# Selective scan on one core: softplus' sum on TensorE, dt's two projections side by side, preparation one group earlier, one more product with B on GpSimd

## The chip, the cores and the metric

The kernel runs on one core of a Trainium2 chip. The time is that of one execution on the device, in microseconds. A core has four engines that compute: TensorE (PE in the profile; its weight loads are PEld), VectorE (DVE), ScalarE (ACT) and GpSimd (POOL). SyncE (SP) issues the DMA transfers here. Each engine takes its instructions in the order in which the program has them, and waits on semaphores for the others.

## What is computed

The input is 2 images of 128 channels and 64 x 64 pixels. Four layers follow each other: attention, a block of deformable convolutions, a residual block of convolutions, and a selective scan (Mamba) over the pixels in four directions. The change lies in the fourth layer. For one direction, with L = 4096 pixels, 256 inner channels and 16 states:

```python
xz = x @ W_in.T;  xh, z = split(xz)
xh = silu(causal_conv4(xh) + conv_b)
x_dbl = xh @ W_xp.T                      # dt (8), B (16), C (16)
dt = softplus(dt @ W_dt.T + b_dt)
h  = exp(dt * A) * h + dt * B * xh       # the scan, for 256 channels x 16 states
y  = (sum over states of h * C + xh * Dp) * silu(z)
out = y @ W_out.T                        # then the fuse over the four directions, and the residual
```

A layernorm over the channels stands ahead of it.

## The kernel before

`layer3` works in 64 blocks (2 images, 4 directions, 8 blocks of 512 pixels each). The 128 partitions of a scan hold 32 channels times 4 states, so a block is cut into 8 groups: two halves of the channels (`hf`) by four quarters of the states (`ng`). A group has four parts `q` of 32 channels each.

For a group k the work is:

- `weights(k)` (L1347): TensorE spreads B's four rows over the partitions, into a PSUM tile `pbc`; the pool `psb` has two such buffers.
- `db_dve(k)` (L1361): VectorE multiplies `pbc` with dt*xh for the first `ND` = 3 of the four parts, into `db` (128 x 1536). `db_pool(k)` (L1368): GpSimd does the fourth (128 x 512), from a copy of B in SBUF that DMAs have spread (`copies`, L1355).
- `expo(k, q)` (L1375): ScalarE forms exp(dt*A) into a PSUM tile `da`, of which there are three buffers; it runs two scans ahead.
- `scan(k, q)` (L1384): VectorE's scan instruction, four in a group. `keep` (L1390) saves the last state on ScalarE.
- `cmul(k, 0)` and `cmul(k, 1)` (L1395): GpSimd multiplies with C, two parts at a time. `sums(k)` (L1401, L1403): TensorE adds the states into `py`. After four groups `gate` (L1412) multiplies with silu(z) on VectorE.

Beside block i's scans the next block is prepared. One iteration of the loop at L1544 is one group ("slot" 0 to 7 in a block), and in each the helpers `transfers`, `front_pe`, `front_act`, `front_pool` and `next_norm` put in their piece. Everything is in program order (`tc.manual_schedule`): the order of these calls is the order of the queues. The pieces, with their slots before:

| piece | engine | slot before |
|---|---|---|
| `begin`: `conv(i+1, 0)`, and `conv(i+1, 1)` (L1261) | TensorE | 6, 7 of the block before |
| `conv_silu` (L1266), with two table loads | ScalarE | 0 |
| `xproj` (L1285), `xproj_copy` (L1291, L1293) | TensorE, ScalarE | 1 |
| `bc_store` (L1297), B and C to DRAM | SP | 2 |
| `delta(0)`, `delta(1)` (L1311): dt's projections, 8 rows each | TensorE | 2, 3 |
| `softplus(0)`, `softplus(1)` (L1317 to L1320): relu(x) and ln(1 + exp(-abs(x))), into two halves of `dd` | ScalarE | 2, 3 |
| `spread(0)`, `spread(1)` (L1325 the sum of the two, L1326 the product with xh) | GpSimd | 3, 4 |
| `xproj_rest`, `rest_copy` (L1303, L1304, L1307) | TensorE, ScalarE | 4 |
| `spread_store` (L1331), `spread_load` (L1340) | SP | 4 and 5; 5 and 0 |
| `zproj` (L1273), `zproj_silu` (L1279), with two table loads | TensorE, ScalarE | 5 |
| `project` (L1420, L1422), `finish` of the block before | TensorE, ScalarE | 3, 4 |
| the layernorm of image 1: `ln_mean` (L1188), `ln_square` (L1199, L1200), `ln_var` (L1204), `ln_scale`, `ln_store` | TensorE, VectorE and ScalarE, TensorE, ScalarE and GpSimd, ScalarE | 6, 7, and 0, 1, 2 of the next block |

The layernorm of image 1 is done beside blocks 22 to 29, one eighth of the image in each. That of image 0 stands ahead of the first block, after some products that prepare weights.

[...]three for `da` (pool `psd`), two for `pbc` (`psb`, which the weight preparation at the layer's start uses too), one for `py`, and two of the pool `psm` (`pm3`), which all other products take in turn, the layernorm's among them. A buffer of a pool is taken in turn, and the writer waits until the reader of its earlier content is done.

Of the kernel before, what the change touches and what calls it, by code (L numbers as in the profile page):

```python
# [10 lines left out]
F32 = mybir.dt.float32  # L11
# [9 lines left out]
P = 128  # L21
NB = 2
HW = 64
L = HW * HW
BLK = 512
NBLK = L // BLK
# [8 lines left out]
DTR = 8  # L35
# [1067 lines left out]
def layer3(g, I, out):  # L1103
# [5 lines left out]
    nc, tc = g.nc, g.tc  # L1109
    NJ = 4  # L1110
    ND = 3
    NNG = N_STATE // NJ
    HB = 3
    with ExitStack() as ctx:
# [8 lines left out]
        nc.sync.dma_start(winz, I["winzT"])  # L1123
        wxp = a.tile([P, 2, 40], F32, name="wxp")
        nc.sync.dma_start(wxp, I["wxpT"])
        wdt = a.tile([40, 2, P], F32, name="wdt")
        nc.sync.dma_start(wdt[32:40], I["wdtT"])
        am = a.tile([P, 2, 4, NNG], F32, name="am")
# [54 lines left out]
        N = {}  # L1183


        def ln_mean(b, k):
            N[k, "mean"] = psm.tile([P, BLK], F32, name="pm3")
            nc.tensor.matmul(N[k, "mean"], onesm, interior(g, b, k * RB, RB), start=True, stop=True)  # L1188
# [13 lines left out]
        def ln_var(b, k):  # L1202
            N[k, "var"] = psm.tile([P, BLK], F32, name="pm3")
            nc.tensor.matmul(N[k, "var"], onesm, N[k, "sq"], start=True, stop=True)  # L1204
# [34 lines left out]
        NBK = len(blocks)  # L1239
        S = {}  # L1240
# [41 lines left out]
        def xproj(i):  # L1282
            S[i]["px"] = px = psm.tile([P, BLK], F32, name="pm3")
            for hf in range(2):
                nc.tensor.matmul(px[:40, :], wxp[:, hf, :], S[i]["u"][:, hf, :], start=(hf == 0), stop=(hf == 1))  # L1285

        def xproj_copy(i):

            px = S[i].pop("px")
            S[i]["xd"] = ck.tile([40, BLK], F32, name="xd", bufs=1)  # L1290
            nc.scalar.copy(S[i]["xd"], px[:40, :])  # L1291
            bc = S[i]["bc"] = ck.tile([4 * N_STATE, BLK], F32R, name="bc")
            nc.scalar.copy(bc[0:32], px[0:32, :])  # L1293
# [12 lines left out]
        def rest_copy(i):  # L1306
            nc.scalar.copy(S[i]["bc"][32:64], S[i].pop("pl")[0:32, :])  # L1307

        def delta(i, hf):
            pdt = S[i]["pdt", hf] = psm.tile([P, BLK], F32, name="pm3")  # L1310
            nc.tensor.matmul(pdt, wdt[32:40, hf, :], S[i]["xd"][32:40], start=True, stop=True)  # L1311

        def softplus(i, hf):
# [43 lines left out]
        def db_dve(k):  # L1357
            i, hf, ng = groups[k]
            x, n = G[k], ND
            x["db"] = wk.tile([P, 4, BLK], F32, name="db")  # L1360
            nc.vector.tensor_tensor(  # L1361
                x["db"][:, :n, :], x.pop("pb").unsqueeze(1).to_broadcast([P, n, BLK]), S[i]["d4", hf][:, 1, :n, :], ALU.mult
            )

        def db_pool(k):
            i, hf, ng = groups[k]
            x, n = G[k], ND
            nc.gpsimd.tensor_tensor(  # L1368
                x["db"][:, n:, :], S[i]["b", ng].unsqueeze(1).to_broadcast([P, 4 - n, BLK]), S[i]["d4", hf][:, 1, n:, :], ALU.mult
            )  # L1370
# [79 lines left out]
        def front_act(i, slot):  # L1450
            if i < NBK:
                if slot == 0:
                    conv_silu(i)
                elif slot == 1:
                    xproj_copy(i)
                elif slot == 2:
                    softplus(i, 0)
                elif slot == 3:
                    softplus(i, 1)
                elif slot == 4:  # L1460
                    rest_copy(i)
                elif slot == 5:
                    zproj_silu(i)


        def transfers(i, slot):
            if i < NBK:
                if slot == 2:
                    bc_store(i)
                elif slot == 4:  # L1470
                    spread_store(i, 0)
                elif slot == 5:
                    spread_load(i, 0)
                    spread_store(i, 1)
            if slot == 0 and i - 1 < NBK:
                spread_load(i - 1, 1)
            for x, ahead in (("b", 3), ("c", 1)):
                j, ng = divmod(8 * (i - 1) + slot + ahead, 8)
                if ng < NNG and 0 < j < NBK:
                    copies(j, x, ng)  # L1480

        def front_pe(i, slot):
            if i < NBK:
                if slot == 1:
                    xproj(i)
                elif slot == 2:
                    delta(i, 0)
                elif slot == 3:
                    delta(i, 1)
                elif slot == 4:  # L1490
                    xproj_rest(i)
                elif slot == 5:
                    zproj(i)
            if i + 1 < NBK:
                if slot == 6:
                    begin(i + 1)
                elif slot == 7:
                    conv(i + 1, 1)
# [5 lines left out]

        LN = {6: ln_mean, 7: ln_square, 8: ln_var, 9: ln_scale, 10: ln_store}

        def next_norm(i, slot):

            for j, s in ((i, slot), (i - 1, slot + 8)):
                b, k = divmod(j, 4 * NBLK)  # L1510
                k -= 4 * NBLK - 2 - NBLK
                if j >= 0 and b + 1 < NB and 0 <= k < NBLK and s in LN:
                    LN[s](b + 1, k)

        with tc.manual_schedule():
# [3 lines left out]
            for t in range(NBLK + 1):  # L1519
                for s in LN:  # L1520
                    if 0 <= t - s // 8 < NBLK:
                        LN[s](0, t - s // 8)
            begin(0)
            conv(0, 1)
            for slot in range(8):
                front_pe(0, slot)
                front_act(0, slot)
                front_pool(0, slot)
# [15 lines left out]
            for k in range(len(groups) + 6):  # L1544
# [129 lines left out]
def _arrays(i):  # L1674
# [26 lines left out]
    for d, (n, s) in enumerate((("offx", slice(0, 9)), ("offy", slice(9, 18)))):  # L1701
# [5 lines left out]
    wxp = l3["W_xp"]  # L1707
    wxp = np.concatenate([wxp[DTR:], wxp[:DTR]])
    a = {
# [9 lines left out]
        "winzT": l3["W_in"][2 * P :].reshape(2, P, P).transpose(2, 0, 1),  # L1719
        "wxpT": wxp.reshape(40, 2, P).transpose(2, 1, 0),  # L1720
        "wdtT": l3["W_dt"].reshape(2, P, DTR).transpose(2, 0, 1),
# [23 lines left out]
```

## Time and profile before

| | us |
|---|---|
| median of 3 runs | 6007.57 |
| lowest and highest | 5999.1, 6009.02 |
| the profiled execution, its time | 6003.65 |
| the profiled execution, its span | 6001.9 |

In the profiled execution the first scan starts at about 2555 us; the 64 blocks take the rest, some 3450 us. Over the span the engines are busy: TensorE 5221.0 us, VectorE 4554.2, ScalarE 3807.3, GpSimd 3701.6.

How to read the views: in the table of groups a row gives line, engine, operation, output<-input with partitions x elements, count, then busy time in us and the mean ns of one, then the idle time of the engine just ahead of these instructions and what ended it. An fp32 product is recorded as two matmul instructions. In the timeline the first two numbers are start and duration in us, "x2" the number of instructions merged, and the bracket is the idle time ahead of them with its releaser. The chain of waits lists start, duration and what ran.

### The profile page before, as it was taken

How to read it: one execution, taken by the hardware profiler on the slowest of the kernel's cores; microseconds unless marked ns; L12 is line 12 of the kernel's file. 1: busy time of each engine (PE TensorE's matmuls, PEld its weight loads, DVE VectorE, ACT ScalarE, POOL GpSimd, SP SyncE). 2: the span in 40 equal slices, each digit the busy share in tenths (PEclk: the TensorE clock that was granted, in tenths of full speed). 3: DMA queues.
4: the chain of work that ended last, by engine and by line, in shares of the span. 5: the costliest groups of instructions: out<-in, count | busy, mean ns of one | idle time of the engine just before them, and what ended most of it. 6: DMA issues, size and time to landing. Idle time of an engine off the chain costs nothing.

```text
span 6001.9 us, 60094 instructions
## 1 busy us (share of the span) xinstructions
PE 5221.0 (87%) x18726; PEld 1662.7 (28%) x18726; DVE 4554.2 (76%) x4262; ACT 3807.3 (63%) x5867; POOL 3701.6 (62%) x2108
## 2 busy tenths in 40 slices
PE   6999999989978689888998888888898888887877
PEld 3333333334444334212222222222222222222221
DVE  5333333355134698499999999999999999999999
ACT  3888888840035411377777766777777777777765
POOL 5111111100010121199999999999999999999999
PEclk9999999999988899888888888888888888888887
DMA  5000001020066200165665556655665556655564
GB/s 152 18 18 18 18 18 32 1 58 1 15 111 110 51 7 0 28 144 135 145 144 133 138 134 145 143 131 135 150 145 132 141 132 145 145 134 137 135 151 106
DMA packets 373049, 575.61 MB, mean 96 GB/s; under 512 B 91080, under 2 KB 145744, under 8 KB 371632
## 3 DMA queue, kind: packets, MB, share of 16 engines
q1 hardware_dynamic: 367408, 563.94, 40.6%
q10 hardware_dynamic: 5312, 7.76, 0.5%
q8 instruction: 149, 2.44, 0.2%
q14 instruction: 180, 1.47, 0.1%
HBM read 482.34 MB, written 89.13 MB: 95 GB/s over the span
## 4 chain that ended last, share of the span: by engine, by line
DVE 45%; PE 38%; DMA 4%; issue 4%; POOL 4%; ACT 2%; SPq 2%; DVEq 0%; ACTq 0%; POOLq 0%
DVE db L1384 31%; DVE db L1361 11%; PE ps L269 10%; PE acc L285 8%; PE m L1034 5%; PE m L548 4%; DMA dd<-dx 2%; POOL db L1395 2%; PE acd L794 2%; PE pm L1261 1%; PE m L508 1%; DVE gt L1412 1%; PE pf L757 1%; PE py L1403 1%; PE pc L645 1%
## 5 line engine op out<-in xcount | busy, mean ns | idle before, releaser
L1395 POOL TENSOR_TENSOR db<-db,c 128x1024 f32<-128x1024 f32 x1024 | 2401.0, 2360 | 80.7 <-ACT hl L1390 67.5
L1384 DVE TENSOR_TENSOR_SCAN db<-da,hl,db 128x512 f32<-128x512 f32 x1792 | 2158.2, 1265 | 53.8 <-ACT da L1375 7.3
L1375 ACT ACTIVATE da<-dd,am 128x512 f32<-128x512 f32 x2048 | 1406.7, 689 | 918.0 <-DVE db L1384 904.0
L275 ACT ACTIVATE e<-ps 128x1024 f16<-128x1024 f32 x1024 | 992.3, 1021 | 134.8 <-PE ps L269 117.7
L1403 PE MATMUL py<-db,fold 128*32 128x512 f32 x4096 | 831.0, 686 | 203.4 <-POOL db L1395 202.9
L1361 DVE TENSOR_TENSOR db<-pbc,dd 128x1536 f32<-128x1536 f32 x512 | 888.2, 1735 | 51.1 <-DMA c<-bx 51.1
L1261 PE MATMUL pm<-xn,wcs 128*128 128x512 f32 x1024 | 722.8, 857 | 30.6 <-DVE xc L1199 17.6
L296 DVE RECIPROCAL rec<-acc 32x512 f32<-32x512 f32 x64 | 214.9, 3358 | 639.6 <-PE acc L285 612.1
L303 POOL TENSOR_TENSOR parts<-parts 32x512 f32<-32x512 f32 x64 | 80.6, 1259 | 975.3 <-DVE parts L302 975.3
L1368 POOL TENSOR_TENSOR db<-b,dd 128x512 f32<-128x512 f32 x512 | 651.2, 1272 | 21.1 <-DMA c<-bx 14.9
L269 PE MATMUL ps<-q,k 32*128 32x512 f32 x4096 | 656.4, 643 | 3.6 <-DVE flag L232 2.8
L285 PE MATMUL acc<-e,v 128*128 128x512 f16 x2048 | 531.3, 382 | 0.0
L1034 PE MATMUL m<-v,u 128*128 128x512 f32 x864 | 376.4, 598 | 51.6 <-DVE v L1003 51.6
L1401 PE MATMUL py<-u,ddp 128*128 128x512 f32 x256 | 183.6, 806 | 232.1 <-DVE gt L1412 231.8
L1347 PE MATMUL pbc<-bc,sel 64*128 64x512 f32 x512 | 284.2, 555 | 83.7 <-DVE db L1361 77.5
L1403 PEld LDWEIGHTS py<-db,fold 128*32 128x32 f32 x4096 | 115.1, 113 | 805.2 <-POOL db L1395 517.5
L1261 PEld LDWEIGHTS pm<-xn,wcs 128*128 128x128 f32 x1024 | 203.6, 209 | 428.8 <-issue 375.8
L1384 DVE TENSOR_TENSOR_SCAN db<-da,db 128x512 f32<-128x512 f32 x256 | 293.3, 1205 | 9.0 <-ACT da L1375 0.7
L285 PEld LDWEIGHTS <-v 128*128 128x128 bf16 x2048 | 158.5, 97 | 510.0 <-issue 388.7
L269 PEld LDWEIGHTS ps<-q,k 32*128 32x128 f32 x4096 | 229.7, 183 | 228.0 <-issue 147.2
L1347 PEld LDWEIGHTS pbc<-bc,sel 64*128 64x128 f32 x512 | 104.8, 205 | 607.6 <-DVE db L1361 306.3
L548 PE MATMUL m<-comb,w 64*128 64x512 f32 (+4 forms) x1296 | 269.9, 575 | 0.0
(311 smaller groups left out, 5734.9 us busy)
## 6 DMA issues: line engine op xcount, KB each, us to landing
dd<-dx SPq DMA_DIRECT2D x1024, 256.0 KB, 6.6
dx<-dd SPq DMA_DIRECT2D x128, 512.0 KB, 7.2
b<-bx SPq DMA_DIRECT2D x1024, 64.0 KB, 5.3
c<-bx SPq DMA_DIRECT2D x1024, 64.0 KB, 2.1
hats<-pos SPq DMA_DIRECT2D x136, 256.0 KB, 9.8
q<-qd SPq DMA_DIRECT2D x32, 512.0 KB, 8.6
w<-in_conv0T SPq DMA_DIRECT2D x18, 288.0 KB, 8.8
xa<-in_x SPq DMA_DIRECT2D x8, 512.0 KB, 9.1
```

Source lines behind the costliest of these rows:

```text
L269: nc.tensor.matmul(ps[:, i, :], k4[h % 2][rows, kb // 4, :], q4[h % 2][rows, qb * BLK : (qb + 1) * BLK], start=True, stop=True,)
L275: nc.scalar.activation(e[:, :n, :], ps[:, :n, :], AF.Exp)
L285: nc.tensor.matmul(acc, v3[b][:, kb, h, :], e[:, i, :], start=(kb == 0), stop=(kb == NS - 1))
L548: yield lambda q=q, dy=dy, src=src, i0=i0, i1=i1: nc.tensor.matmul(m[:, i0 * NF : i1 * NF], w[half, dy, q, x, :], src, start=(dy == KC and ...
L1034: nc.tensor.matmul(m[x], weights[j][:, dy, x, :], v[j][b][:, x, r0 : r0 + RP, :].rearrange("p r i -> p (r i)"), start=(dy == 0), stop=(dy ...
L1261: nc.tensor.matmul(shaped(blk, pu), wcs[:, hf, s, :], window(blk, sgn * s), start=(s == 0), stop=(s == 3))
L1361: nc.vector.tensor_tensor(x["db"][:, :n, :], x.pop("pb").unsqueeze(1).to_broadcast([P, n, BLK]), S[i]["d4", hf][:, 1, :n, :], ALU.mult)
L1368: nc.gpsimd.tensor_tensor(x["db"][:, n:, :], S[i]["b", ng].unsqueeze(1).to_broadcast([P, 4 - n, BLK]), S[i]["d4", hf][:, 1, n:, :], ALU.mult)
L1375: nc.scalar.activation(da, S[i]["d4", hf][:, 0, q, :], AF.Exp, scale=am[:, hf, q, ng : ng + 1])
L1384: nc.vector.tensor_tensor_scan(d1, d0, d1, 0.0 if first else hl[:, hf, ng, q, :], ALU.mult, ALU.add)
L1395: nc.gpsimd.tensor_mul(v, v, S[i]["c", ng].unsqueeze(1).to_broadcast([P, 2, BLK]))
L1403: nc.tensor.matmul(S[i]["y", hf][32 * q : 32 * q + 32, :], fold, G[k]["db"][:, q, :], start=False, stop=(ng == NNG - 1),)
```

## The change

1. `softplus`' two parts are no longer added by GpSimd. `sum_parts` adds them with two products with the identity on TensorE into a `pm3` tile, and `sum_copy` copies it back to `dd` on ScalarE. `spread` keeps the product with xh alone.
2. `W_xp`'s dt rows stand twice in the prepared weights, so that `xproj` gives dt in rows 32 to 39 and again in 64 to 71. `delta(0)` uses the first, `delta(1)` the second, and both are issued in one slot.
3. Preparation is shifted by one group: `conv` to slots 5 and 6, `conv_silu` to 7, `xproj` and `xproj_copy` to 0, `bc_store`, both `delta`s and `softplus(0)` to 1, `sum_parts(0)`, `softplus(1)` and `sum_copy(0)` to 2, `sum_parts(1)`, `sum_copy(1)`, `xproj_rest` and `rest_copy` to 3, `zproj` to 4. `project` and `finish` both go to slot 5, ahead of the preparation.
4. The layernorm's `mean` and `var` tiles come from `psb` (`pbc`) instead of `psm`, and its steps lie in slots 0, 1, 3, 4 and 5 of one block.
5. In the last group of a block (`hf` = 1, `ng` = 3) GpSimd does two of the four products with B instead of one, and VectorE two instead of three.

```diff
-    ND = 3
+    ND = ((3, 3, 3, 3), (3, 3, 3, 2))
...
-        wxp = a.tile([P, 2, 40], F32, name="wxp")
+        wxp = a.tile([P, 2, 72], F32, name="wxp")
         nc.sync.dma_start(wxp, I["wxpT"])
-        wdt = a.tile([40, 2, P], F32, name="wdt")
-        nc.sync.dma_start(wdt[32:40], I["wdtT"])
+        wdt = a.tile([72, P], F32, name="wdt")
+        for hf in range(2):
+            nc.sync.dma_start(wdt[32 + 32 * hf : 40 + 32 * hf], I["wdtT"][:, hf])
...
         def ln_mean(b, k):
-            N[k, "mean"] = psm.tile([P, BLK], F32, name="pm3")
+            N[k, "mean"] = psb.tile([P, BLK], F32, name="pbc")
...
         def ln_var(b, k):
-            N[k, "var"] = psm.tile([P, BLK], F32, name="pm3")
+            N[k, "var"] = psb.tile([P, BLK], F32, name="pbc")
...
-                nc.tensor.matmul(px[:40, :], wxp[:, hf, :], S[i]["u"][:, hf, :], start=(hf == 0), stop=(hf == 1))
+                nc.tensor.matmul(px[:72, :], wxp[:, hf, :], S[i]["u"][:, hf, :], start=(hf == 0), stop=(hf == 1))
...
-            S[i]["xd"] = ck.tile([40, BLK], F32, name="xd", bufs=1)
-            nc.scalar.copy(S[i]["xd"], px[:40, :])
+            S[i]["xd"] = ck.tile([72, BLK], F32, name="xd", bufs=1)
+            nc.scalar.copy(S[i]["xd"], px[:72, :])
...
-            nc.tensor.matmul(pdt, wdt[32:40, hf, :], S[i]["xd"][32:40], start=True, stop=True)
+            r = slice(32 + 32 * hf, 40 + 32 * hf)
+            nc.tensor.matmul(pdt, wdt[r], S[i]["xd"][r], start=True, stop=True)
...
+        def sum_parts(i, hf):
+            ps = S[i]["dt", hf] = psm.tile([P, BLK], F32, name="pm3")
+            for x in range(2):
+                nc.tensor.matmul(ps, g.ident, S[i]["dd", hf][:, x, :], start=(x == 0), stop=(x == 1))
+
+        def sum_copy(i, hf):
+            nc.scalar.copy(S[i]["dd", hf][:, 0, :], S[i].pop(("dt", hf)))
+
         def spread(i, hf):
...
-            nc.gpsimd.tensor_add(dd[:, 0, :], dd[:, 0, :], dd[:, 1, :])
             nc.gpsimd.tensor_mul(dd[:, 1, :], dd[:, 0, :], s_["u"][:, hf, :])
...
-            x, n = G[k], ND
+            x, n = G[k], ND[hf][ng]
...
         def front_act(i, slot):
             if i < NBK:
                 if slot == 0:
-                    conv_silu(i)
+                    xproj_copy(i)
                 elif slot == 1:
-                    xproj_copy(i)
+                    softplus(i, 0)
                 elif slot == 2:
-                    softplus(i, 0)
+                    softplus(i, 1)
+                    sum_copy(i, 0)
                 elif slot == 3:
-                    softplus(i, 1)
+                    sum_copy(i, 1)
+                    rest_copy(i)
                 elif slot == 4:
-                    rest_copy(i)
-                elif slot == 5:
                     zproj_silu(i)
+            if i + 1 < NBK and slot == 7:
+                conv_silu(i + 1)
...
-                if slot == 2:
+                if slot == 1:
                     bc_store(i)
...
         def front_pe(i, slot):
             if i < NBK:
-                if slot == 1:
+                if slot == 0:
                     xproj(i)
+                elif slot == 1:
+                    delta(i, 0)
+                    delta(i, 1)
                 elif slot == 2:
-                    delta(i, 0)
+                    sum_parts(i, 0)
                 elif slot == 3:
-                    delta(i, 1)
+                    sum_parts(i, 1)
+                    xproj_rest(i)
                 elif slot == 4:
-                    xproj_rest(i)
-                elif slot == 5:
                     zproj(i)
             if i + 1 < NBK:
-                if slot == 6:
+                if slot == 5:
                     begin(i + 1)
-                elif slot == 7:
+                elif slot == 6:
                     conv(i + 1, 1)
...
-        LN = {6: ln_mean, 7: ln_square, 8: ln_var, 9: ln_scale, 10: ln_store}
+        LN = {0: ln_mean, 1: ln_square, 3: ln_var, 4: ln_scale, 5: ln_store}
...
+                if i >= 1 and i <= NBK:
+                    if slot == 5:
+                        project(i - 1)
+                        finish(i - 1)
                 front_pe(i + 1, slot)
                 front_act(i + 1, slot)
                 front_pool(i + 1, slot)
-                if i >= 1 and i <= NBK:
-                    if slot == 3:
-                        project(i - 1)
-                    elif slot == 4:
-                        finish(i - 1)
                 if live:
                     next_norm(i, slot)
```

More of the change, by code (lines that the diff above doesn't have):

```diff
@@ L1366, in db_pool @@
             i, hf, ng = groups[k]
-            x, n = G[k], ND
+            x, n = G[k], ND[hf][ng]
             nc.gpsimd.tensor_tensor(
@@ L1503, in front_pool @@
                     spread(i, slot - 3)
-        LN = {6: ln_mean, 7: ln_square, 8: ln_var, 9: ln_scale, 10: ln_store}
+        LN = {0: ln_mean, 1: ln_square, 3: ln_var, 4: ln_scale, 5: ln_store}
         def next_norm(i, slot):
[L1509 to L1513, printed above, removed]
+            b, k = divmod(i, 4 * NBLK)
+            k -= 4 * NBLK - 2 - NBLK
+            if b + 1 < NB and 0 <= k < NBLK and slot in LN:
+                LN[slot](b + 1, k)
         with tc.manual_schedule():
@@ L1520, in layer3 @@
                 for s in LN:
-                    if 0 <= t - s // 8 < NBLK:
-                        LN[s](0, t - s // 8)
+                    if 0 <= t - s // 3 < NBLK:
+                        LN[s](0, t - s // 3)
             begin(0)
             conv(0, 1)
+            conv_silu(0)
             for slot in range(8):
@@ L1707, in _arrays @@
     wxp = l3["W_xp"]
-    wxp = np.concatenate([wxp[DTR:], wxp[:DTR]])
+    wxp = np.concatenate([wxp[DTR:], wxp[:DTR], np.zeros((24, wxp.shape[1]), np.float32), wxp[:DTR]])
     a = {
@@ L1719, in _arrays @@
         "winzT": l3["W_in"][2 * P :].reshape(2, P, P).transpose(2, 0, 1),
-        "wxpT": wxp.reshape(40, 2, P).transpose(2, 1, 0),
+        "wxpT": wxp.reshape(72, 2, P).transpose(2, 1, 0),
         "wdtT": l3["W_dt"].reshape(2, P, DTR).transpose(2, 0, 1),
```

## The prediction

> **What bounds the kernel now.** I began with the busy time by window. The selective scan fills the time from about 2550 us to the end; two of its windows:
>
> ```profile
> core 0: us, PE busy (x) PEld busy (x) DVE busy (x) ACT busy (x) POOL busy (x), PEclk, DMA share, GB/s
> 3000.00:3500.00 500.00, 435.74 (x1080) 105.80 (x1079) 492.04 (x394) 357.71 (x640) 487.73 (x266) 0.86 0.58 138
> 4000.00:4500.00 500.00, 434.81 (x1084) 109.91 (x1076) 486.26 (x390) 354.62 (x639) 485.32 (x267) 0.85 0.60 143
> ```
>
> VectorE and GpSimd are both busy 97 to 98% of it, so this view alone cannot say which one sets the pace. The chain that ended last, over one block of eight groups, can:
>
> ```profile
> by line: DVE db L1384 64.3%; DVE db L1361 29.8%; issue 5.1%; DVE gt L1412 4.2%; DVEq L1361 0.4%; DVEq L1384 0.3%
> ...
> 5735.93 0.58 DVE gt L1412
> 5736.52 1.68 DVE db L1361
> ...
> 5738.28 2.07 DVE db L1384 x2
> 5740.35 0.31 issue
> 5740.66 2.43 DVE db L1384 x2
> 5743.09 1.66 DVE db L1361
> ...
> 5744.84 2.07 DVE db L1384 x2
> ```
>
> It never leaves VectorE. A group is four scans and one product with B: from 5738.28 to 5744.84, 6.56 us. A block is 8 x 6.56 + 2 x 0.58 (gates) = 53.64 us, and by the starts of the gate rows, read over the whole scan, the blocks follow each other every 53.74 us, nearly all of them. What VectorE loses is lost to the end, what it saves is saved. Next come the groups' rows:
>
> ```profile
> L1395 POOL TENSOR_TENSOR db<-db,c 128x1024 f32<-128x1024 f32 x1024 | 2401.0, 2360 | 80.7 <-ACT hl L1390 67.5
> L1375 ACT ACTIVATE da<-dd,am 128x512 f32<-128x512 f32 x2048 | 1406.7, 689 | 918.0 <-DVE db L1384 904.0
> L1361 DVE TENSOR_TENSOR db<-pbc,dd 128x1536 f32<-128x1536 f32 x512 | 888.2, 1735 | 51.1 <-DMA c<-bx 51.1
> L1368 POOL TENSOR_TENSOR db<-b,dd 128x512 f32<-128x512 f32 x512 | 651.2, 1272 | 21.1 <-DMA c<-bx 14.9
> ```
>
> ScalarE idles 904 us behind VectorE (904/64 = 14 us a block). But how late ScalarE may be at one point is another question; one block of the timeline of VectorE and ScalarE shows it:
>
> ```profile
> 4230.62 0.69 ACT L1266 ACTIVATE u<-pm,vecs 128x512 f32<-128x512 f32 x1 [3.13 <-PE pm L1261]
> ...
> 4233.35 2.46 DVE L1384 TENSOR_TENSOR_SCAN db<-da,hl,db 128x512 f32<-128x512 f32 x2 [3.20 <-ACT da L1375]
> ```
>
> There ScalarE waited 3.13 us for a convolution, and VectorE lost 3.20 us. So **the exps run only two scans ahead**: where ScalarE's extra work for the next block already fills the gap, a wait of ScalarE goes to VectorE in full.
>
> **The skill.** The Trainium skill, page "TensorE: Matmul & The Clock Gate", Part 1, says that the array's clock drops to half after idle time and comes back after some 3.4 us of work. The trace agrees on the halving (how long the return takes it doesn't show): the same dt projection, before and after a stretch with idle gaps of about 1.6 us:
>
> ```profile
> 4072.21 1.12 PE L1311 MATMUL pm<-xd,wdt 8*128 8x512 f32 x2
> ...
> 4080.32 0.79 PE L1347 MATMUL pbc<-bc,sel 64*128 64x512 f32 x1
> 4081.03 2.07 PE L1311 MATMUL pm<-xd,wdt 8*128 8x512 f32 x2
> ```
>
> The same page (head table and Part 3) says that matmuls stay in order, and that ScalarE, VectorE and GpSimd are strict FIFOs; the rows above agree (exps wait behind the late silu). "TensorEngine Tiling (Array Packing)", Overview, has products of few rows on different row groups run together; no run so far shows the two deltas so. "GPSIMD Engine Reference", section 1, has GpSimd contend with VectorE instructions that read two SBUF inputs; db_dve and the scans read one of theirs from PSUM, so I add nothing; no row so far shows it either way.
>
> **The change, part by part.**
>
> *One more product with B on GpSimd.* In one group of eight, db_dve shrinks from 128x1536 to 128x1024. Its slope, from 1735 ns and the gate's 665 ns for 512 elements (timeline rows of L1412), is 1070/1024 = 1.045 ns an element, so 0.535 us a block, on the path: 64 x 0.535 = **-34.2 us**. GpSimd's part grows from 1.272 to 2.36 us (the 128x1024 row), +1.09. It is now due at the third scan instead of the fourth, but db_pool runs a group ahead (5745.31 to 5746.58 for a fourth scan at about 5755), so it has 5 us and more.
>
> *Softplus' sum.* Off GpSimd: two adds of 1.273, -2.55 a block; with the above, -1.46 a block. It was not the bound: nothing gained. Onto TensorE: four fp32 products of 0.92 (the convolution's eight instructions, four products, take 3.70 when warm) = 3.7 us a block. Its bracketed idle times in the block of 5709 to 5763 sum to 10.6, and these cover it. Onto ScalarE: two copies of 0.59 (row L1433), 1.2 of its 14 us. In group 2 it does softplus (2.43) and one copy (0.59), 3.0 in all, less than the 3.87 of conv_silu with two table loads, which delays a scan by 0.06 us today.
>
> *dt's projections side by side.* Two products of 1.05 in one group instead of two; at best 1.0 us of TensorE saved, at worst none; both lie in idle time. xproj with 72 instead of 40 columns streams the same 512 columns, and its copy the same 512 elements: nothing.
>
> *Preparation a group earlier.* conv, conv_silu, xproj_copy, softplus, rest_copy and zproj_silu each come one group sooner, with their producer still one group ahead (or in the same group, as xproj and zproj were). SP's queue: bc_store one group sooner behind its copy; spread_store and all loads (L1340, L1355) keep their groups, behind stores that are ready no later: nothing. project and finish go from groups 3 and 4 to 5, both: TensorE then has project 2.8, begin's convolution 3.7, ddp and sums 3 and weights 0.5 = 10 us in a group of 6.56, a lag of 3.5 us that groups 6 and 7 (5.4 and 1.7) take up before conv_silu and before the weights are due. finish ends some 6 us into the group; the next exp is due at 8.3.
>
> *The layernorm's mean and variance into pbc's two buffers.* This is what I expect to decide. In blocks 22 to 29 (eight blocks) mean comes in group 0 and variance in group 3, each between two weights. With two buffers, mean takes that of the next group's weights, free only when db_dve reads it at the end of the group; and **the weights issued in the group after take the buffer of the weights before mean, free only at the end of that group**. Behind those weights on TensorE stand delta (group 1) and zproj (group 4), and for these ScalarE waits, with the next exps behind it. Before, both lay in psm, and those blocks took 54.6 us (53.74 and the 0.68 of L1199).
>
> Group 1, from its first scan: scans 4.72, gate 0.58, product 1.75: buffer free at 7.05. Weights and first delta, TensorE idle for 4 to 5 us here and in group 4, and thus probably cold: 0.05 + 0.75 + 2.0; warm 0.05 + 0.45 + 1.1. Then softplus 2.43, Square 0.54, exp 0.69: exp at 13.5 cold, 12.3 warm. VectorE wants it at 7.8 + 2.4 = 10.2 (with the layernorm's subtraction). Stall 3.3 or 2.1.
>
> Group 4: buffer free at 6.47; weights 0.8 or 0.5; two products of zproj 3.6 or 1.95; second silu 0.55, table load 1.30, Ln 0.70, Exp 0.53, exp 0.69: 14.6 or 12.7. VectorE wants it at 6.56 + 2.4 = 8.96. Stall 5.7 or 3.7.
>
> Together 9.0 cold, 5.8 warm. I take 8.0, since the last products may be warm again: 8 x 8.0 = **+64 us** (46 to 72).
>
> *The start.* mean now waits behind the weight preparation in the same two buffers (its first product at 2473.65 so far; the preparation's TensorE part is reached at 2480), against a chain whose first variance began at 2480.32: about +2.7. Softplus' last sum goes over TensorE and ScalarE (0.92 to 2 twice, 0.59) instead of an add of 1.27: +1.2 to 3.3. One more DMA of wdt on SP ahead of wfu, which the chain passes: 0.43, within these. **+4.5 us** (2 to 7). At the end project waits for the last gate as before: nothing.
>
> Sum: -34.2 + 64 + 4.5 = +34. Against the profiled execution's 6003.65 us (span 6001.9) that is 6038; the median of the runs, 6007.57, stands 3.9 higher, so 6041.
>
> **The rivals.** (1) *The stall is covered.* If ScalarE's slack or TensorE's lead absorbs the new wait, only the product and the start remain: 6007.6 - 34 + 4.5 = 5978, faster. It decides below (34.2 - 4.5)/8 = 3.7 us of stall per normalising block. For it: the 14 us of ScalarE idle a block. Against it: block 4205 to 4262 above, 3.13 us of wait and 3.20 of loss. (2) *It cancels*: a stall about 4 us, TensorE warm and the Square ahead: 6007.6 - 34 + 32 + 4.5 = 6010. (3) *TensorE becomes the bound* in ordinary blocks: it runs cold part of the time (mean clock 0.85), and the lag of group 5, doubled, could reach conv_silu; 1 us in each of 56 ordinary blocks would be 6041 + 56 = 6097. Against it: 10.6 us idle a block. (4) *The change doesn't do what it says*: the sum on TensorE leaves GpSimd 1.5 us more idle and VectorE as it was; that is in the sum already.
>
> **How the numbers follow.** My case 0.71, mostly 6018 to 6052; rival 1 0.13; rival 2 0.10; rival 3 0.06. Of the likeliest case 0.03 fall within 0.2%, about what a measurement of this kernel can tell from no change (6007.6 +- 12). So slower 0.74, same 0.13, faster 0.13. Leaving out rival 3 and most of rival 1, the range is 5996 to 6062; the likeliest case's own is 6018 to 6052.
>
> **What would show it.** Ordinary blocks 53.2 us from gate to gate, L1361's groups of 128x1024 near 1.2 us. Eight blocks near 62 us, with weights (pbc) waiting for db_dve, softplus and silu waiting for TensorE just after, and two stalls of VectorE behind exps, of about 3 and 5 us. I am wrong if those blocks stay below 57 us, or if ordinary ones exceed 53.7.

## The result, and the profile after

The changed kernel takes 6090.04 us (median of 4 runs, 6085.78 to 6091.52) against 6005.65 (4 runs, 5999.1 to 6009.02): a ratio of 1.0141, 95% interval 1.0123 to 1.0158. The forecast was +34 us; it became +84, beyond the end of the range. Its profiled execution took 6090.28 us (span 6088.5), so the two traces differ by 86.6 us of span.

Busy time by window, the first view of the prediction again, for the changed kernel (the columns are the engines' busy time and instructions):

```profile
core 0: us, PE busy (x) PEld busy (x) DVE busy (x) ACT busy (x) POOL busy (x), PEclk, DMA share, GB/s
3000.00:3500.00 500.00, 424.59 (x1155) 109.30 (x1148) 482.95 (x391) 363.73 (x655) 471.64 (x245) 0.90 0.57 138
4000.00:4500.00 500.00, 405.50 (x1073) 109.46 (x1072) 452.00 (x366) 341.54 (x621) 443.14 (x234) 0.87 0.53 130
```

VectorE was busy 492 and 486 us of these stretches; now it is busy 483 and 452. The engine that set the pace has idle time of 17 us in the first window and 48 us in the second, which holds about half of the layernorm's blocks. The change made VectorE's work smaller and made VectorE wait.

What it waits for is seen in the row of its scans, first before the change, then after it:

```profile
L1384 DVE TENSOR_TENSOR_SCAN db<-da,hl,db 128x512 f32<-128x512 f32 x1792 | 2158.2, 1265 | 53.8 <-ACT da L1375 7.3
```

```profile
L1394 DVE TENSOR_TENSOR_SCAN db<-da,hl,db 128x512 f32<-128x512 f32 x1792 | 2160.5, 1265 | 144.4 <-ACT da L1385 97.6
```

The scans take as long as before, but wait 98 us for ScalarE's exps instead of 7; the 256 scans without an earlier state wait another 15 us (before 0.7). ScalarE's waits have grown as well. More groups of the changed kernel, each shape apart (count | busy, mean ns | idle before, by releaser):

```profile
L1405 POOL TENSOR_TENSOR db<-db,c 128x1024 f32<-128x1024 f32 x1024 | 2401.3, 2358 | 160.4 <-ACT hl L1400 155.5 <-DMA dd<-dx 2.4 <-PE pm L1328 2.0
L1385 ACT ACTIVATE da<-dd,am 128x512 f32<-128x512 f32 x2048 | 1401.9, 689 | 849.7 <-DVE db L1394 845.6 <-DMA c<-bx 0.4
L1371 DVE TENSOR_TENSOR db<-pbc,dd 128x1536 f32<-128x1536 f32 x448 | 778.0, 1737 | 56.0 <-DMA c<-bx 56.0
L1371 DVE TENSOR_TENSOR db<-pbc,dd 128x1024 f32<-128x1024 f32 x64 | 76.7, 1199 | 0.0
L1268 ACT ACTIVATE u<-pm,vecs 128x512 f32<-128x512 f32 x128 | 84.4, 686 | 55.0 <-PE pm L1263 54.3
L1320 ACT ACTIVATE dd<-pm,vecs 128x512 f32<-128x512 f32 x128 | 85.8, 670 | 45.6 <-PE pm L1314 45.6
L1281 ACT ACTIVATE z<-pm 128x512 f32<-128x512 f32 x128 | 70.4, 595 | 39.1 <-PE pm L1275 38.5
```

The smaller product is there, at the forecast size: 64 of 1199 ns beside 448 of 1737. The last three rows are what has grown: conv_silu waits 54 us in all for the convolution (before 16), softplus 46 us for the deltas (before 11), and the silu of z 39 us for zproj (before 1).

Read from gate to gate, the 63 intervals between blocks fall into three kinds. Starts of the first half's gates, in us (the forecast puts the product's 0.535 into every interval):

| stretch | before | after | difference | forecast |
|---|---|---|---|---|
| span's start to first gate | 2591.2 | 2603.0 | +11.8 | +4.5 |
| 28 intervals, preparing a column block | 1503.0 | 1519.9 | +16.9 | -15.0 |
| 8 intervals with the second image's layernorm | 434.6 | 507.4 | +72.8 | +59.7 |
| the 27 others | 1448.9 | 1432.7 | -16.2 | -14.4 |
| last gate to the end | 24.3 | 25.5 | +1.2 | 0 |

Of the 27 others 25 prepare a row block, and two the first column blocks of the second image; they are called row intervals below. Row intervals follow each other every 53.21 us (median; before 53.74), the forecast's 53.2. Column intervals take 54.28 (median; before 53.74). Layernorm intervals take 63.43 on average (before 54.32).

**A layernorm block**, first VectorE's, then TensorE's and ScalarE's rows of its timeline (start, duration, and in brackets the idle time before and its releaser):

```profile
3769.15 2.46 DVE L1394 TENSOR_TENSOR_SCAN db<-da,hl,db 128x512 f32<-128x512 f32 x2 [3.65 <-ACT da L1385]
...
3794.83 2.46 DVE L1394 TENSOR_TENSOR_SCAN db<-da,hl,db 128x512 f32<-128x512 f32 x2 [5.89 <-ACT da L1385]
```

```profile
3762.68 0.76 PE L1357 MATMUL pbc<-bc,sel 64*128 64x512 f32 x1 [3.31 <-DVE db L1371]
3763.37 2.08 PE L1314 MATMUL pm<-xd,wdt 8*128 8x512 f32 x4
...
3786.43 0.79 PE L1357 MATMUL pbc<-bc,sel 64*128 64x512 f32 x1 [4.44 <-DVE db L1371]
3787.15 3.78 PE L1275 MATMUL pm<-xn,winz 128*128 128x512 f32 x4
```

```profile
3765.48 0.69 ACT L1320 ACTIVATE dd<-pm,vecs 128x512 f32<-128x512 f32 x1 [5.64 <-PE pm L1314]
3789.26 0.60 ACT L1281 ACTIVATE z<-pm 128x512 f32<-128x512 f32 x1 [3.68 <-PE pm L1275]
```

This is the chain of the forecast, twice: weights wait for db_dve, deltas (L1314) and zproj (L1275) stand behind them, softplus (L1320) and silu (L1281) wait for those, and the exps behind them come 3.65 and 5.89 us late to a scan. The products after the idle time run slowly: zproj takes 3.78 us here and 1.98 in the row blocks.

**A column block**, which the forecast had not looked at, TensorE's rows, then ScalarE's and VectorE's:

```profile
2869.47 0.49 PE L1357 MATMUL pbc<-bc,sel 64*128 64x512 f32 x1 [1.00 <-DVE db L1371]
2869.90 2.16 PE L1430 MATMUL pm<-xa,ident 128*128 128x512 f32 x2
2871.88 1.90 PE L1432 MATMUL pm<-gt,mt 128*128 128x512 f32 x4
2873.62 7.03 PE L1263 MATMUL pm<-xn,wcs 128*128 128x512 f32 x8
...
2882.44 0.49 PE L1357 MATMUL pbc<-bc,sel 64*128 64x512 f32 x1
2882.86 7.12 PE L1263 MATMUL pm<-xn,wcs 128*128 128x512 f32 x8
...
2890.91 0.49 PE L1357 MATMUL pbc<-bc,sel 64*128 64x512 f32 x1
```

```profile
2890.02 0.69 ACT L1268 ACTIVATE u<-pm,vecs 128x512 f32<-128x512 f32 x1 [0.95 <-PE pm L1263]
```

```profile
2892.74 2.46 DVE L1394 TENSOR_TENSOR_SCAN db<-da,hl,db 128x512 f32<-128x512 f32 x2 [1.01 <-ACT da L1385]
```

In the first two directions of each image the window is a transposed view of xn, and each half of the convolution (four products) takes 7.1 us, not the 3.70 of a row block. Project stands ahead of it with 4 us. The second half ends at 2889.98; the second silu had been ready for it 0.95 us earlier, and VectorE loses 1.01 us.

### The profile page after: what moved, and what is told of

It reads as the page before. It is cut to its first block, busy times and chain, and to the rows that moved or that the text cites. A ratio compares the mean times of both kernels' runs of the same rounds, so it can differ in the third digit from the quotient of the medians.

```text
span 6088.5 us, 61321 instructions
## 1 busy us (share of the span) xinstructions
PE 5237.0 (86%) x19238; PEld 1713.3 (28%) x19238; DVE 4523.5 (74%) x4262; ACT 3862.8 (63%) x5995; POOL 3611.1 (59%) x1980
## 4 chain that ended last, share of the span: by engine, by line
PE 46%; DVE 37%; ACT 6%; issue 4%; DMA 2%; POOL 2%; SPq 1%; DVEq 0%; ACTq 0%; POOLq 0%
DVE db L1394 25%; PE ps L269 10%; DVE db L1371 10%; PE acc L285 8%; PE pm L1263 7%; PE m L1034 5%; PE m L548 4%; PE acd L794 2%; ACT da L1385 2%; PE pm L1430 1%; PE pm L1432 1%; PE m L508 1%; PE pf L757 1%; DVE gt L1422 1%; PE pbc L1357 1%
## 5 line engine op out<-in xcount | busy, mean ns | idle before, releaser
L1371 DVE TENSOR_TENSOR db<-pbc,dd 128x1536 f32<-128x1536 f32 (+1 forms) x512 | 854.7, 1669 | 56.0 <-DMA c<-bx 56.0
L1413 PE MATMUL py<-db,fold 128*32 128x512 f32 x4096 | 770.7, 687 | 139.6 <-POOL db L1405 139.5
L1378 POOL TENSOR_TENSOR db<-b,dd 128x512 f32<-128x512 f32 (+1 forms) x512 | 719.7, 1406 | 58.4 <-DVE db L1394 41.4
L1263 PE MATMUL pm<-xn,wcs 128*128 128x512 f32 x1024 | 686.7, 819 | 4.8 <-ACT xn L1216 4.8
L1411 PE MATMUL py<-u,ddp 128*128 128x512 f32 x256 | 198.6, 868 | 213.9 <-DVE gt L1422 213.9
L1413 PEld LDWEIGHTS py<-db,fold 128*32 128x32 f32 x4096 | 109.4, 115 | 718.2 <-POOL db L1405 447.5
L1328 PE MATMUL pm<-dd,ident 128*128 128x512 f32 x512 | 292.2, 699 | 0.9 <-ACT dd L1321 0.9
```

The lines of the kernel that those rows point to most:

```text
L1263: nc.tensor.matmul(shaped(blk, pu), wcs[:, hf, s, :], window(blk, sgn * s), start=(s == 0), stop=(s == 3))
L1371: nc.vector.tensor_tensor(x["db"][:, :n, :], x.pop("pb").unsqueeze(1).to_broadcast([P, n, BLK]), S[i]["d4", hf][:, 1, :n, :], ALU.mult)
L1378: nc.gpsimd.tensor_tensor(x["db"][:, n:, :], S[i]["b", ng].unsqueeze(1).to_broadcast([P, 4 - n, BLK]), S[i]["d4", hf][:, 1, n:, :], ALU.mult)
L1413: nc.tensor.matmul(S[i]["y", hf][32 * q : 32 * q + 32, :], fold, G[k]["db"][:, q, :], start=False, stop=(ng == NNG - 1),)
```

## The experiments

The theory is that there are three losses, against the product's gain: the layernorm's tiles in pbc's buffers, project ahead of the strided convolution, and the start. Each is taken away by itself, then the parts are recombined. Times are medians, and ratios are to the kernel before, which ran beside each set (6005.4 to 6006.9 us). The layernorm's old groups put its eight intervals one later; they are averaged there.

### e_ln_slots: the layernorm in its old groups

```
-LN = {0: ln_mean, 1: ln_square, 3: ln_var, 4: ln_scale, 5: ln_store}
+LN = {6: ln_mean, 7: ln_square, 8: ln_var, 9: ln_scale, 10: ln_store}
 (next_norm and the loop at the start as in the kernel before)
```

> The changed kernel with the layernorm's five steps back in groups 6 to 10 (mean in group 6, variance in group 0 of the next block), their two PSUM tiles still in pbc's buffers. Theory (the wait of weights for a pbc buffer costs time where ScalarE needs what stands behind those weights on TensorE): behind mean stand only the weights of group 7 and sums, which nobody needs for a group, so that stall is gone; behind variance stand the weights of group 1 and the deltas, so a stall of about 3.6 us stays. Eight layernorm blocks fall from 63.4 to about 57 us, the whole to about 6042 us. Rival A (the stall comes from the two buffers whatever stands behind them): blocks stay at 62 to 64 us, 6090. Rival B (the stall comes from ScalarE's new order in these groups alone): blocks at 53.9, 6015.

Measured: 6074.83 us, ratio 1.0113 (1.0096 to 1.0130), layernorm intervals 61.70. That is just below rival A's 62 to 64 and far from the theory's 57: most of the loss has stayed. VectorE's waits and TensorE's rows of one such block:

```profile
3866.36 2.34 DVE L1394 TENSOR_TENSOR_SCAN db<-da,db 128x512 f32<-128x512 f32 x2 [0.19 <-ACT da L1385]
...
3884.60 2.34 DVE L1394 TENSOR_TENSOR_SCAN db<-da,db 128x512 f32<-128x512 f32 x2 [4.89 <-ACT da L1385]
...
3901.05 2.34 DVE L1394 TENSOR_TENSOR_SCAN db<-da,db 128x512 f32<-128x512 f32 x2 [3.71 <-ACT da L1385]
```

```profile
3891.25 1.92 PE L1413 MATMUL py<-db,fold 128*32 128x512 f32 x4 [2.49 <-POOL db L1405]
3893.10 0.79 PE L1357 MATMUL pbc<-bc,sel 64*128 64x512 f32 x1
3893.82 3.78 PE L1328 MATMUL pm<-dd,ident 128*128 128x512 f32 x4
```

Mean behind the convolution costs almost nothing (0.19), as the theory has it, and against rival A. Variance still costs the deltas (4.89). But a second stall has come, two groups later: the products with C are late on GpSimd, TensorE's sums (L1413) wait for those, and behind the sums stands the new sum of softplus' parts (L1328), for whose copy ScalarE waited 4.78 us. The products with C are late for two reasons: the scans before them were late, and on GpSimd the layernorm's own product (L1212), which stands ahead of them, had waited 9.32 us for ScalarE's Exp until 3884.06. In this kernel ScalarE now depends on GpSimd by way of TensorE, so one stall makes another. Rival B fell.

### e_ln_psm: old groups and the old buffers

```
-N[k, "mean"] = psb.tile([P, BLK], F32, name="pbc")     (and "var")
+N[k, "mean"] = psm.tile([P, BLK], F32, name="pm3")
 (with e_ln_slots' edits)
```

> The changed kernel with the layernorm in its old groups (mean in group 6, variance in group 0 of the next block) and its tiles back in pm's buffers, for both images. Theory (it is weights waiting behind the layernorm's tiles for pbc, with ScalarE's operands behind the weights, that costs the layernorm blocks their time): no weights wait, layernorm blocks at 54 to 55.5 us (53.2, the subtraction's 0.68 and up to 1.6 for mean, which now waits in group 6 for conv_silu in group 7), start 6.8 us sooner as with the first image's tiles alone; the whole at 6010 to 6022 us. Rival F (with the sum on TensorE any layernorm product among the preparation makes ScalarE late, as the third group's sum_copy did with the old groups in pbc): blocks at 58 us or more, the whole at 6042 or more.

Measured: 6029.58 us, ratio 1.0040 (1.0026 to 1.0055); layernorm intervals 57.26. The buffers and groups together were 60 of the 84 us (the start's 6.3 of e_start, below, among them): the theory holds in the main, though its 54 to 55.5 us a block was missed by about 2, and its 6010 to 6022 us by 8. Against e_ln_slots, from which it differs by the buffers alone, the layernorm intervals fell by 4.4 us each. The new groups with pm's buffers were not run, so what the groups alone cost stays open. The rest of the layernorm's loss is seen in two waits of VectorE's timeline:

```profile
3848.35 0.69 DVE L1201 TENSOR_TENSOR xc<-xa,pm 128x512 f32<-128x512 f32 x1 [2.07 <-PE pm L1190]
...
3889.78 0.69 DVE L1422 TENSOR_TENSOR gt<-py,z 128x512 f32<-128x512 f32 x1 [3.69 <-PE pm L1432]
```

Mean (L1190), now in pm's buffers, waits for conv_silu and the subtraction waits for mean; and the gate waits for project (L1432), moved to group 5, to release one of two gt buffers. Over the whole scan these are 16.6 us in 8 waits and 11.5 us in 6, about what the eight blocks still lose.

### e_project: project and finish out of group 5

```
-if slot == 5: project(i - 1); finish(i - 1)     (ahead of front_pe)
+if slot == 0: project(i - 2); finish(i - 2)     (behind front_act; gt bufs=3)
```

> The changed kernel with project and finish taken out of group 5, where they stand ahead of the next block's convolution, and put behind xproj and its copy in group 0 of the block after. Theory (in the column directions the convolution's strided products take 7.1 us instead of 3.7, and project ahead of them makes TensorE late for conv_silu in group 7): the column blocks fall from 54.28 to 53.2 us, about 27 x 1.07 = -29 us, the whole to about 6061 us; layernorm blocks stay at 63.4. Rival C (the loss in column blocks comes from the two sums on TensorE and their copies on ScalarE): column blocks stay at 54.3, the whole at 6090.

Measured: 6072.42 us, ratio 1.0107 (1.0090 to 1.0124). Column intervals fall to 53.21 us, and their sum from 1519.9 to 1486.5, by 33.4 us. Rival C fell: both sums and their copies are still there. TensorE and ScalarE in the same column block:

```profile
2866.98 7.12 PE L1263 MATMUL pm<-xn,wcs 128*128 128x512 f32 x8
2876.31 7.12 PE L1263 MATMUL pm<-xn,wcs 128*128 128x512 f32 x8
```

```profile
2885.47 1.27 ACT L1268 ACTIVATE u<-pm,vecs 128x512 f32<-128x512 f32 x2
```

The convolution is as slow as before, but ends at 2883.4, two us ahead of the silu. The whole gained only 17.6 us of the expected 29: layernorm intervals rose to 64.91 on average (a third stall of 3.08 us in the block read), row intervals lost 5 us in all, and the layers before this one ended 2.7 us later in this execution.

### e_contig: the convolution reads contiguous pixels

```
-nc.tensor.matmul(shaped(blk, pu), wcs[:, hf, s, :], window(blk, sgn * s), ...)
+nc.tensor.matmul(pu, wcs[:, hf, s, :], flat(xns[b])[:, f0 : f0 + BLK], ...)
```

> The changed kernel with the convolution reading contiguous pixels in every direction: it leaves out the transposed window of the two column directions, so those directions scan other data. Theory (the strided window is what makes these products slow, and this is what lets the lag reach conv_silu): four products near 3.7 us in the column directions too, column blocks at 53.2 us, the whole at about 6061 us. Rival D (project in group 5 is enough by itself, or the strided zproj and residual product): column blocks stay at 54.0 or more, 6080 or more. Rival C (sums and copies): no change, 6090.

Measured: 6043.41 us, ratio 1.0062 (1.0045 to 1.0079). Its column directions scan other data, so only its time is of use. TensorE's rows, a column block:

```profile
2857.36 3.60 PE L1263 MATMUL pm<-xn,wcs 128*128 128x512 f32 x8
2863.18 3.70 PE L1263 MATMUL pm<-xn,wcs 128*128 128x512 f32 x8
```

3.70 instead of 7.12 us with no other change: the strided window is what makes these products slow. Column intervals: 53.21, with project still in group 5. So it takes both, project in front and the strided window; either repair is enough for these intervals, and rival D fell. The whole gained 18 us more than expected. 10.6 us of that lie ahead of the first gate, most of them where the 16 instructions of the next block's convolution stand ahead of the first weights (7.05 instead of 13.93 us); the kernel before has them there too.

### e_start: the first image's layernorm in pm's buffers

```
+N[k, "mean"] = psm.tile(..., name="pm3") if b == 0 else psb.tile(..., name="pbc")     (and "var")
```

> The changed kernel with the first image's layernorm tiles back in pm's buffers, the second image's left in pbc's. Theory (at the start the means queue behind the weight preparation in pbc's two buffers): first gate about 8 us sooner, the whole at about 6082 us; about 3.5 us of the start's 11.8 stay, for the sum of softplus' parts before the first scan. Rival E (the start's loss is all in the sum and its copies, or in the DMA of wdt): no change, 6090.

Measured: 6080.60 us, ratio 1.0127 (1.0110 to 1.0144). The layers before end at times that differ by several us from run to run, so the start is counted from their last ScalarE instruction: the first gate comes 118.0 us after it in the kernel before, 130.5 in the changed one, 124.2 here. So 6.3 us of the start are means waiting behind the weight preparation; the theory's 8 was near, rival E fell. Another 3.8 lie between the first convolution and the first weights: 44.1 us changed, 40.3 before, 40.2 in e_add, which has no sums on TensorE. Of the 2.4 us that are left, 2.1 lie ahead of the first convolution. What is left there is no more than executions with the same instructions up to there differ by: e_two_alone comes 1.8 us later than the kernel before, and e_add 3.3 later than the changed one.

### e_three and e_two_alone: the product by itself

```
e_three (changed kernel):     ND = ((3, 3, 3, 3), (3, 3, 3, 3))
e_two_alone (kernel before):  ND = ((3, 3, 3, 3), (3, 3, 3, 2))
```

> The changed kernel with three products with B on VectorE in all groups, as before. Theory (VectorE sets the pace of row blocks, ScalarE behind TensorE that of column blocks and layernorm blocks): the 0.535 us return in full in about 29 row blocks (53.2 to 53.74) and in part where ScalarE is late: the whole at 6106 to 6124 us. Rival (the product was hidden all the same): 6090.

Measured: 6107.30 us, ratio 1.0165 (1.0149 to 1.0182), 17.3 us above the changed kernel. By kind: +12.4 in row intervals, +1.6 in column intervals, +2.9 with the layernorm. In the changed kernel the product was worth half of its 34 us, since in the other intervals VectorE mostly waited for ScalarE, however little it had to do.

> The kernel before with the one more product with B on GpSimd and nothing else. Theory (the sum had to leave GpSimd first): GpSimd's work in a block is 8 x (2 x 2.36 + 1.27) + 2 x (1.27 + 1.27) + 1.09 = 54.1 us by its rows, over VectorE's 53.2, so GpSimd sets the pace: ordinary blocks at 54.1 to 54.6, the whole at 6030 to 6060 us. Rival G (GpSimd's work is bounded by less, or VectorE sets the pace all the same): ordinary blocks at 53.2, the whole at 5973 us.

Measured: 5990.56 us, ratio 0.9972 (0.9960 to 0.9983): faster. My theory fell. Busy time by window, and GpSimd's timeline:

```profile
3000.00:3500.00 500.00, 441.54 (x1081) 107.71 (x1081) 489.51 (x396) 358.92 (x642) 498.43 (x267) 0.89 0.58 139
```

```profile
5682.97 1.28 POOL L1325 TENSOR_TENSOR dd<-dd 128x512 f32<-128x512 f32 x1
...
5696.31 1.28 POOL L1368 TENSOR_TENSOR db<-b,dd 128x512 f32<-128x512 f32 x1
5697.54 4.66 POOL L1395 TENSOR_TENSOR db<-db,c 128x1024 f32<-128x1024 f32 x2
5702.17 2.35 POOL L1368 TENSOR_TENSOR db<-b,dd 128x1024 f32<-128x1024 f32 x1
...
5725.44 2.37 POOL L1395 TENSOR_TENSOR db<-db,c 128x1024 f32<-128x1024 f32 x1 [1.03 <-ACT xd L1291]
...
5737.16 1.29 POOL L1325 TENSOR_TENSOR dd<-dd 128x512 f32<-128x512 f32 x1
```

GpSimd is at 498 of 500 us, but its rows overlap: the one at 5697.54 starts 1.23 us after a row of 1.28, and two of 2.36 fill 4.63. From the first add of a block (5682.97) to that of the next (5737.16) are 54.19 us with 1.03 of waiting, so 53.16 of work, where I had added durations to 54.1. GpSimd and VectorE then tie at 53.2, and ordinary intervals are at 53.20 to 53.25 (medians). The sum did not have to leave GpSimd for this product. But the tie has its price: 15 of the 34 us came, not all, and rival G's 5973 was missed by 18. VectorE's waits for exps rose from 8.0 to 22.4 us; what makes the exps late there was not followed.

### e_add: the sum back on GpSimd

```
-sum_parts(i, hf) on TensorE, sum_copy(i, hf) on ScalarE
+nc.gpsimd.tensor_add(dd[:, 0, :], dd[:, 0, :], dd[:, 1, :])     (in spread)
```

> The changed kernel with softplus' two parts added by GpSimd again and neither the two sums on TensorE nor their copies on ScalarE. Theory (the sum costs and gains nothing by itself; GpSimd then has as much work a block as VectorE, both 53.2 us, as the product alone on the kernel before showed): row blocks at 53.2 to 53.5, column blocks at 54.3 (project ahead of the strided convolution is still there), layernorm blocks at 62 to 64; the whole within 10 us of 6090. Rival C (sums and copies make the column or layernorm blocks late): column blocks at 53.2 or layernorm blocks at 60 or less, the whole at 6060 or less.

Measured: 6095.99 us, ratio 1.0146 (1.0129 to 1.0163); column intervals 54.28, layernorm 63.49, row 53.21. The stalls of the column and layernorm blocks are the same without the sums on TensorE, as the theory has it, and rival C falls here too. The whole is 6 us longer than with them: the intervals together are 10 us longer, most of it in row intervals, and the first gate comes 4.5 us sooner, 3.9 of it because the layers before ended sooner. So in these blocks the sum on TensorE cost nothing, and saved a little.

### e_fix, e_fix2 and e_more: the repairs together

e_fix is e_project and e_ln_psm in one, with finish's last copy in a buffer of its own (it shared "sq" with the layernorm). e_fix2 differs from it by the second image's mean, which stays in pbc's buffers. e_more adds one product with B:

```
-ND = ((3, 3, 3, 3), (3, 3, 3, 2))
+ND = ((3, 3, 3, 2), (3, 3, 3, 2))
```

> The changed kernel with both repairs: project and finish behind xproj in group 0 of the block after next (three gt buffers), and the layernorm in its old groups and in pm's buffers. Theory: from 6090, -30 in the column blocks, -4 at the start (-6.8 + 2.7), and of the layernorm blocks' 73 all but 6 to 16: 5988 to 6000 us, faster than both kernels. Rival F (the layernorm's products still make ScalarE late): 6010 or more.

Measured: 6000.61 us (20 runs), ratio 0.9991 (0.9984 to 0.9997): barely faster than the kernel before, and just past the slow end of the expected span. Column intervals 53.20, layernorm 56.65, where the subtraction again waits 2.07 us for mean:

```profile
3783.00 0.69 DVE L1201 TENSOR_TENSOR xc<-xa,pm 128x512 f32<-128x512 f32 x1 [2.07 <-PE pm L1190]
```

> Both repairs as before, with the second image's mean (in group 6) in pbc's buffers and only its variance in pm's. Theory (with mean in pm, it waits on TensorE for conv_silu, and VectorE's subtraction waited 2.07 us for it; with mean in pbc only weights stand behind it, which nobody needs for a group): layernorm blocks fall from 56.3 to about 54 us, the whole from 6000.6 to about 5982 us. Rival (the weights that wait for mean make xproj or project late): layernorm blocks at 56 or more, the whole at 5998 or more.

Measured: 5984.97 us, ratio 0.9964 (0.9950 to 0.9978); layernorm intervals 54.81. As expected, but for 0.8 us a block: single stalls of up to 3.1 us behind exps are left.

> The kernel with both repairs and mean in pbc, and a second product with B on GpSimd in each block, now that the sum has left it: db_dve takes two products in the last group of each half. Theory (VectorE sets the pace, GpSimd has 2.5 us of room): VectorE's block falls by another 0.535 us to 52.68, GpSimd's is 46.9 + 2.5 + 2 x 1.08 = 51.6 us by starts, so ordinary blocks at 52.7 and the whole some 32 us under the kernel with both repairs, about 5950 us. Rival (ScalarE or TensorE is late once VectorE is quicker, or GpSimd sets the pace): ordinary blocks stay above 53, the whole at 5970 or more.

Measured: 5971.19 us, ratio 0.9938 (0.9922 to 0.9955), the fastest of all. Ordinary intervals are at 52.68, as the theory has it. The whole, though, lies in the rival's span, and the forecast of it was missed by 21 us: layernorm intervals rose to 56.56 (+14 us), since a quicker VectorE finds ScalarE later, and row intervals kept single stalls. The rival's reason, a ScalarE that is late once VectorE is quicker, holds for these blocks. The window of e_more shows VectorE and GpSimd almost level:

```profile
3000.00:3500.00 500.00, 438.92 (x1176) 113.94 (x1174) 490.28 (x401) 366.40 (x662) 491.99 (x250) 0.92 0.59 142
```

With the sum on GpSimd, a second product would put GpSimd at 53.16 + 1.08 = 54.2 us a block by its starts, over VectorE's 52.7 (an estimate; it was not run). The room for the second product is what the sum on TensorE is good for; the first fits without it, if tightly.

## Why the prediction was wrong, point by point

- **The layernorm's buffers**: the mechanism, both places and VectorE's order were right; the size was short. I gave 9.0 us cold and 5.8 warm and took 8.0, "since the last products may be warm again". The stalls were 3.65 + 5.89 = 9.54 in the block shown, and 9.6 on average by the intervals ((72.8 + 4.3) / 8), a little over the cold ends (3.3 + 5.7). What failed in this term is the reason for taking less: the products behind the wait were not warm again (2.08 us for the deltas and 3.78 for zproj, against 1.13 and 1.98 in row blocks). That is 13 us of the 52 by which the two traces miss the forecast.
- **Project in group 5**: this is the step that failed, and the largest part of the miss. I put its cost at nothing: I summed group 5 to "10 us", a lag "that groups 6 and 7 (5.4 and 1.7) take up before conv_silu", with every duration from one block of a row direction (5709 to 5763), the convolution's 3.7 us among them. In the column block shown, TensorE works 13.0 us for group 5 (from its weights at 2869.47 to the next at 2882.44) and 8.5 for group 6 (to 2890.91), 21.5 us where two groups of VectorE last some 13, and the lag does reach conv_silu. The kernel before has the slow convolution too, and its own timeline shows it:

```profile
2810.18 7.12 PE L1261 MATMUL pm<-xn,wcs 128*128 128x512 f32 x8
2818.65 7.12 PE L1261 MATMUL pm<-xn,wcs 128*128 128x512 f32 x8
```

  It cost nothing there: project was three groups earlier, and conv_silu (at 2827.49) did not wait. Rival 3, at a chance of 0.06, had the path right, the lag of group 5 reaching conv_silu, and its size of 1 us a block (54.28 - 53.21 = 1.07). Its reason, a TensorE that runs cold part of the time, was not it: in e_contig the same products at the same place take 3.60 and 3.70 us. It also priced 56 blocks, and 28 intervals show it, so that its total, 6097, lies near 6090 by luck. Against the forecast the failed step made 32 us: 17 of loss, and 15 of the product's gain that could not show. e_project and e_contig show both of its halves.
- **The product**: -34.2 was right for VectorE's work (1737 to 1199 ns), and row intervals fell by 0.53 (median). But my sum added it to the stalls as if the two were independent. Where ScalarE is late, VectorE's saving only lengthens its wait: e_three shows 17 us, not 34.
- **The start**: +4.5 forecast, 11.8 measured, of which about 6.3 for the means (2.7 forecast) and 3.8 for the sum (1.2 to 3.3 forecast); the rest is of the size by which executions with the same instructions differ there. Both terms were too small.
- **What was put at nothing**: the sum of softplus' parts on TensorE and ScalarE cost nothing in ordinary blocks (e_add), as forecast. It was not free everywhere: in the layernorm blocks of e_ln_slots it carried a stall on. Of the "at best 1.0 us" of TensorE for the deltas side by side, all came: the four instructions take 1.13 us, where one pair alone took 1.12.

```profile
5712.60 1.13 PE L1314 MATMUL pm<-xd,wdt 8*128 8x512 f32 x4
```

  The Trainium skill's page "TensorEngine Tiling (Array Packing)", Tiling Modes, says that different tiles of the array (here two groups of rows) can run their products in parallel; this trace agrees. On the time it was worth nothing, as forecast.
- **What would show it**: I had named ordinary blocks over 53.7 us as a sign of error. Of the 55 ordinary intervals 26 were over it, most of them at 54.28.

## What to carry to other kernels

Before moving a step, read the queue it joins in every kind of block that the loop has; the same line can take twice as long in another direction, and slack read in one block is not slack in all. In a queue that keeps its order, ask for each new wait what stands behind it and who needs that soon: weights that nobody needs for a group may wait, the deltas behind them may not. A saving on the engine that sets the pace counts only in stages where it sets the pace after the change.

## What the hardware showed that was not expected

- Four fp32 products of 512 columns take 3.70 us with a contiguous moving operand and 7.12 with the transposed window (e_contig against the changed kernel). The identity product shows the same: 2.16 us on the column view of xa, 1.13 in the row blocks. The runs show the cost of the transposed window, not what in TensorE or memory causes it.
- GpSimd's rows overlap by some 0.05 us when they follow each other, so summed durations overstate its block by about one us in 54; starts give 53.16. That was enough to turn a tie into the loss that I had forecast for e_two_alone.
- The time from the end of the layers before to this layer's first gate differs by 2 us between executions with the same instructions up to there (118.0 in the kernel before, 120.0 in e_two_alone), the time to its first convolution by 3.3 (e_add against the changed kernel), and the layers before end up to 8 us apart. No run here says why.
